# Reordering what stands ahead of the first attention scores in a transformer block with adaptive layer norm

## The chip, the cores and the metric

The kernel runs on one core of a Trainium2 chip. The metric is device time in microseconds (us) for one execution of the whole block, given as the median of several runs. A profiled execution has a span (first to last instruction) and a time of its own, which is a little longer than the span.

## The reference

Input x is 8 x 1024 x 256 in float32. The block computes, per batch:

```python
mod = (silu(c) @ wmod).reshape(8, 6, 1, 256)      # c: 8 x 256
sa, ca, ga, sb, cb, gb = ...                      # six rows; ga, gb kept at 0.25 or more in size
h = layernorm(x) * (1 + ca) + sa
x = x + ga * attention(h, w_qkv, w_o)             # 16 heads of 64, softmax over 1024 keys
h = layernorm(x) * (1 + cb) + sb
x = x + gb * ffn(h)                               # 8 experts, each takes its 512 best tokens
```

Only `h` of the first batch, its first projections (q, k, v) and the modulation rows stand ahead of the first attention scores, and the change is about these.

## The kernel before, in words

Attention is cut into units `u`: one batch, one pair of heads, one half of the queries (512). A unit has four groups `g`, and in each group two blocks of 128 keys are handled: TensorE makes the scores (`s`, L356), ScalarE copies them to SBUF (`p`, L365), VectorE keeps a running maximum (`top`, L370). At the end of the unit the maximum is turned (`tt`, L377), reduced and split in parts (L385 to L393), turned back (`pn`, L399) and spread (`less`, L412); in later groups VectorE subtracts it, ScalarE takes exp, TensorE multiplies with v (`av`, L427) and GpSimd adds up the denominators.

The order of every engine's instructions is written out by hand. `at(g, where, f, ...)` puts a small task into a group, and a loop over `g` (from -16 before) emits, for each group, loads, scores, the tasks of "m1", exp and values, and then the tasks of "m2". Small tasks are the projections `qk_task` (`pq`, L321, evicted by ScalarE to `qk`) and `v_task` (`pv`, L338), the turning of the normalised rows `ln_out` (`ptx`), `mod_rows` (`pr`, L229: four of the six rows of modulation, needed only much later), and the tasks of later stages. Groups below zero are the fill: no scores run there.

PSUM has four pools: `ps_s` with two tiles of two banks (tag "s", for scores and `tt`), `ps_b` (`less`), `ps_av` (`av`), and `ps_m` with one bank (tag "mm") which all small tasks share, one after the other. A tile is not written while another engine reads it, and the next task in a bank waits for the eviction of the one before.

Ahead of the loop stand the loads and the modulation. `c` (8 x 256), `wm0` (the third of wmod for sa and ca), and the rows of x of the first batch (two halves, `x_first`) are loaded on the SP queue; the weights of the first four heads (`wq0`, six loads of 128 KB) on ScalarE's queue; `late_loads` then puts the other heads' weights (`wq1`, six loads of 384 KB), the rest of wmod, w_o and small tensors on SP. A DMA takes one of eight semaphores in turn, and where one is used again the queue waits until the DMA that had it before has landed. `mod_silu` computes silu(c) from an exp on ScalarE and three operations on VectorE on 8 x 256, turns it in two blocks to `sT`, and `mod_columns` multiplies it with wm0 (`pm`, L215) into `modT`. `ln_first(t)` takes the statistics of 256 rows (VectorE, then a power on GpSimd) and normalises them on VectorE (L281). `ln_out` turns them with 16 passes of a matmul with the identity and evicts on VectorE, with modT as scale and shift (L300). `steps_of` is a small table used near the end of the kernel.

Of the kernel before, what the change touches and what calls it, by code (L numbers as in the profile page):

```python
# [32 lines left out]
ALU = mybir.AluOpType  # L33
# [9 lines left out]
def adaln_block(  # L43
# [51 lines left out]
    scores = const.tile([P, KT, E, NTT // KT], F32, name="scores")  # L95
    modT = const.tile([P, 2 * KC, B], F32, name="modT")


    steps_of = const.tile([P, 16, 4], I32, name="steps_of")
    nc.gpsimd.memset(steps_of, 0)  # L100
    nc.gpsimd.iota(steps_of[:, 14, :], pattern=[[1, 4]], base=0, channel_multiplier=0)
    for s in range(14):
        nc.vector.tensor_scalar(
            steps_of[:, s, :], steps_of[:, 14, :], 28 - 2 * s, None, op0=ALU.logical_shift_left
        )

    mod_d = dram.tile([B, 3 * D], F32, name="mod_d")
    gb_d = dram.tile([B, D], F32, name="gb_d")
# [45 lines left out]
    def wq_load(eng, i, a):  # L154
        heads = slice(0, H0) if i == 0 else slice(H0, H)
        for k in range(KC):
            eng.dma_start(
                wqs[i][:, k, a],
                w_qkv[heads, a, k * P : (k + 1) * P, :].rearrange("h p n -> p h n"),
            )  # L160
# [1 line left out]


    c_sb = small.tile([B, D], F32, tag="row", name="c_sb", bufs=6)
    nc.sync.dma_start(c_sb, c)
    wm = [work.tile([P, KC, 2 * D], F32, tag=t, name=f"wm{i}", bufs=n)
          for i, (t, n) in enumerate((("p", PB), ("ot", 2), ("ot", 2)))]

    def wm_load(i):
        nc.sync.dma_start(  # L170
            wm[i], wmod[:, 2 * i * D : 2 * (i + 1) * D].rearrange("(k p) m -> p k m", p=P)
        )

    wm_load(0)
    x_first = []
    for i in range(2):
        t = work.tile([P, NT // 2, D], F32, tag="p", name=f"x_first{i}", bufs=PB)
# [1 line left out]
            t, x[0, i * S // 2 : (i + 1) * S // 2, :].rearrange("(t p) d -> p t d", p=P)  # L179
        )  # L180
        x_first.append(t)
    for a in (2, 1, 0):
        wq_load(nc.scalar, 0, a)

    def late_loads():
        for a in (2, 1, 0):
            wq_load(nc.sync, 1, a)
        for i in (1, 2):
            wm_load(i)
        nc.sync.dma_start(wo, w_o.rearrange("(i p) d -> p i d", p=P))  # L190
        nc.sync.dma_start(rw, router_w.rearrange("(k p) e -> p k e", p=P))
        nc.sync.dma_start(rb, router_b.rearrange("(o e) -> o e", o=1).to_broadcast([P, E]))
        nc.sync.dma_start(b1_sb, b1.rearrange("e (f p) -> p e f", p=P))
# [3 lines left out]
    mod_row = []  # L197

    def mod_silu():
        sig = small.tile([B, D], F32, tag="row", name="sig", bufs=6)  # L200
        nc.scalar.activation(sig, c_sb, AF.Exp, scale=-1.0)
        nc.vector.tensor_scalar_add(sig, sig, 1.0)
        nc.vector.reciprocal(sig, sig)
        nc.vector.tensor_mul(sig, c_sb, sig)
        for k in range(KC):
            pt = ps_m.tile([P, B], F32, tag="mm", name=f"pt{k}")
            nc.tensor.transpose(pt, sig[:, k * P : (k + 1) * P], ident[:B, :B])
            nc.vector.tensor_copy(sT[:, k, :], pt)

    def mod_columns():  # L210

        pm = ps_m.tile([P, 2 * KC, B], F32, tag="mm", name="pm")
        for m in range(2 * KC):
            for k in range(KC):
                nc.tensor.matmul(  # L215
                    pm[:, m, :], wm[0][:, k, m * P : (m + 1) * P], sT[:, k, :],
                    start=(k == 0), stop=(k == KC - 1),
                )
        nc.vector.tensor_copy(modT[:, :KC, :], pm[:, :KC, :])
        nc.vector.tensor_scalar_add(modT[:, KC:, :], pm[:, KC:, :], 1.0)  # L220
# [31 lines left out]
    def at(g, where, f, *args):  # L252
        steps.setdefault((g, where), []).append((f, args))
# [5 lines left out]

    ln_x = {}  # L260

    def ln_load(b, t):
        ln_x[b, t] = small.tile([P, 2, D], F32, tag="lnx", name=f"lnx{b}_{t}", bufs=2)
        nc.sync.dma_start(
            ln_x[b, t], x[b, 2 * t * P : (2 * t + 2) * P, :].rearrange("(i p) d -> p i d", p=P)
        )
# [4 lines left out]
    def ln_first(t):  # L271
        ln_x[0, t] = x_first[t // 2][:, 2 * (t % 2) : 2 * (t % 2) + 2, :]
        ln_stats(0, t)
        ln_norm(0, t)

    def ln_norm(b, t):
        xt, mv = ln_x[b, t]
        rs = rstd_of(small, mv, 2, f"a{b}_{t}")
        for i in range(2):
            eng = nc.vector if b == 0 else nc.gpsimd  # L280
            eng.tensor_scalar(  # L281
                xt[:, i, :], xt[:, i, :], mv[:, i, 0:1], rs[:, i : i + 1],
                op0=ALU.subtract, op1=ALU.mult,
            )

    def ln_out(b, t):
        if t == 0:
            hTs[b] = work.tile([P, KC, S], F32, tag="hT", name=f"hT{b}")
        xt = ln_x.pop((b, t))[0]
        pt = ps_m.tile([P, KC, 2 * P], F32, tag="mm", name=f"ptx{b}_{t}")  # L290
        for k in range(KC):
            for i in range(2):
                for m in range(2):
                    c0 = k * P + m * N
                    nc.tensor.matmul(
                        pt[m * N : (m + 1) * N, k, i * P : (i + 1) * P],
                        xt[:, i, c0 : c0 + N], ident, start=True, stop=True,
                    )
        for k in range(KC):
            nc.vector.tensor_scalar(  # L300
                hTs[b][:, k, 2 * t * P : (2 * t + 2) * P], pt[:, k, :],
                modT[:, KC + k, b : b + 1], modT[:, k, b : b + 1],
                op0=ALU.mult, op1=ALU.add,
            )

    def ln_task(b, t, g):
        at(g - 4, "load", ln_load, b, t)
        at(g - 2, "post", ln_stats, b, t)
        at(g - 1, "pool", ln_norm, b, t)
        at(g, "m2", ln_out, b, t)  # L310


    def qk_task(b, p, i):
        a, half = (1, i) if i < 2 else (0, i - 2)
        if half == 0:
            qks[b, p, a] = work.tile([P, S], F32, tag="qk"[a], name=f"qk{a}_{b}_{p}")
        pq = ps_m.tile([P, 512], F32, tag="mm", name=f"pq{b}_{p}_{i}")
        sl = slice(half * 512, half * 512 + 512)
        for k in range(KC):
            for m in range(2):  # L320
                nc.tensor.matmul(  # L321
                    pq[m * N : (m + 1) * N, :], wq_of(k, a, 2 * p + m), hTs[b][:, k, sl],
                    start=(k == 0), stop=(k == KC - 1),
                )
        if a == 0:
            nc.scalar.mul(qks[b, p, a][:, sl], pq, scale)  # L326
        else:
            nc.scalar.copy(qks[b, p, a][:, sl], pq)  # L328
# [311 lines left out]
    def free_slot(g, behind=False):  # L640
# [2 lines left out]
        taken.add(g)  # L643
        return g

    for t in range(NT // 2):
        at(-15 + t, "m2", ln_out, 0, t)
        ln_task(1, t, free_slot(39 + 4 * t, True))
    for b in range(B):
        for p in range(NP):  # L650
            P0 = 8 * (b * NP + p)
            for i, g in enumerate((-7, -6, -5, -2)):
                at(P0 + g, "m1", qk_task, b, p, i)
            if p % 2 == 0:
                for t, g in enumerate((-9, -3, -1, 5)):
                    at(P0 + g, "m1", v_task, b, p // 2, t)
            if (b, p) == (B - 1, NP - 1):
                continue

            at(P0 + 17, "load", den_load, b, p)  # L660
            at(P0 + 18, "post", den_inv, b, p)
            at(P0 + 19, "load", den_spread, b, p)
            at(P0 + 20, "pool", den_mul, b, p)
        if b + 1 < B:
            if b + 2 < B:
                for t in range(NT // 2):
                    ln_task(b + 2, t, free_slot(64 * (b + 1) + 39 + 4 * t, True))
            for t in range(NT):
                g = free_slot(64 * (b + 1) + 19 + 4 * t, True)
                at(g - 2, "load", out_load, b, t)  # L670
                at(g, "m2", out_proj, ps_m, b, t)
                at(g + 1, "pool", out_norm, b, t)
                if t % 2:
                    g = free_slot(g + 2, True)
                    at(g, "m2", out_turn, ps_m, b, t - 1)
                    g = free_slot(g + 1)
                    at(g, "m2", out_route, ps_m, b, t - 1)
                    at(g + 1, "post", out_exp, b, t - 1)
                    at(g + 2, "post", out_score, b, t - 1)
                    at(g + 3, "pool", out_store, b, t - 1)  # L680
# [4 lines left out]
    for b in range(B):  # L685
        at(64 * b + 30, "load", gates, b)
    for i in range(2):
        at(-1, "m2", mod_rows, i)
    for t in range(NT):
        at(4 * NSU + (3 if t < NT // 2 else 4), "load", last_load, t)  # L690

    with tc.manual_schedule():
        late_loads()
        mod_silu()
        ln_first(0)
        mod_columns()
        for t in range(1, NT // 2):
            ln_first(t)
        for t in parts_of:
            nc.vector.memset(t, 0.0)  # L700
        g = -16
        while g < 4 * NSU + LAG or steps:
            u, gm = divmod(g, 4)
            run(g, "load")
# [88 lines left out]
                out_store(b, s - 4)  # L793
    assert not steps, sorted(steps)
    attn.close()


    wts = ctx.enter_context(tc.tile_pool(name="ewts", bufs=4))
    ex_w = {}
# [281 lines left out]
```

## Time and profile before

| | |
|---|---|
| median of 3 runs | 3637.75 us (3636.31 to 3641.64) |
| profiled execution, its time | 3636.69 us |
| its span | 3635.0 us |
| mean granted TensorE clock | 0.983 |
| TensorE busy | 3462.8 us (95%) |
| VectorE busy | 2904.0 us (80%) |
| GpSimd busy | 2657.6 us (73%) |
| ScalarE busy | 2432.8 us (67%) |
| first scores on TensorE start | 59.89 us |

Busy time is the time in which an engine has an instruction in work; matmuls overlap, so a busy TensorE is not one at its peak. PE is TensorE, PEld its weight loads, ACT ScalarE, DVE VectorE, POOL GpSimd, SP SyncE (which only issues DMAs). A line of the timeline gives start, length, engine, source line, operation, tiles and number of records; the bracket tells how long the engine was idle before and what ended it. The row of 40 digits gives busy tenths of equal slices of 91 us.

### The profile page before, as it was taken

How to read it: one execution, taken by the hardware profiler on the slowest of the kernel's cores; microseconds unless marked ns; L12 is line 12 of the kernel's file. 1: busy time of each engine (PE TensorE's matmuls, PEld its weight loads, DVE VectorE, ACT ScalarE, POOL GpSimd, SP SyncE). 2: the span in 40 equal slices, each digit the busy share in tenths (PEclk: the TensorE clock that was granted, in tenths of full speed). 3: DMA queues.
4: the chain of work that ended last, by engine and by line, in shares of the span. 5: the costliest groups of instructions: out<-in, count | busy, mean ns of one | idle time of the engine just before them, and what ended most of it. 6: DMA issues, size and time to landing. Idle time of an engine off the chain costs nothing. (4 is left out here: it accounts for less than half of the span.)

```text
span 3635.0 us, 54304 instructions
## 1 busy us (share of the span) xinstructions
PE 3462.8 (95%) x20670; PEld 1460.7 (40%) x20670; DVE 2904.0 (80%) x3651; ACT 2432.8 (67%) x2980; POOL 2657.6 (73%) x1537
## 2 busy tenths in 40 slices
PE   6999999999999999999999999999999999982898
PEld 2333334334433434334433344344334344342565
DVE  4888888888888888888888888888888888857442
ACT  2777777777777777777777777777777777740111
POOL 0778778887788777977788888877888887851232
PEclk9999999999999999999999999999999999995999
DMA  3010011111121122111211112011311112133332
GB/s 76 13 38 29 24 31 57 45 43 41 49 56 38 45 61 55 33 39 45 65 52 30 52 45 62 30 52 43 62 38 43 46 51 56 51 85 122 94 99 41
DMA packets 189653, 185.40 MB, mean 51 GB/s; under 512 B 48952, under 2 KB 167240, under 8 KB 189264
## 3 DMA queue, kind: packets, MB, share of 16 engines
q1 hardware_dynamic: 170736, 160.04, 15.6%
q0 software_dynamic: 7168, 12.72, 1.8%
q10 hardware_dynamic: 11488, 9.18, 0.9%
q8 instruction: 163, 2.67, 0.3%
q14 instruction: 98, 0.80, 0.1%
HBM read 127.06 MB, written 63.21 MB: 52 GB/s over the span
## 5 line engine op out<-in xcount | busy, mean ns | idle before, releaser
L446 POOL TENSOR_TENSOR acc<-acc,p 128x1024 f32<-128x1024 f32 x762 | 1805.2, 2369 | 361.8 <-ACT p L418 328.5
L365 ACT COPY p<-s 128x1024 f32<-128x1024 f32 x1024 | 996.2, 1018 | 421.1 <-PE s L356 414.5
L415 DVE TENSOR_TENSOR p<-p,less 128x1024 f32<-128x1024 f32 x1024 | 1206.7, 1210 | 32.8 <-PE less L412 30.0
L370 DVE TENSOR_TENSOR top<-top,s 128x1024 f32<-128x1024 f32 x768 | 936.9, 1220 | 259.9 <-ACT p L365 218.2
L418 ACT ACTIVATE p<-p 128x1024 f32<-128x1024 f32 x1024 | 1041.7, 1057 | 75.0 <-DVE p L415 74.7
L356 PE MATMUL s<-qk,qk 64*128 64x512 f32 x4096 | 1024.9, 612 | 36.1 <-DVE parts L393 32.3
L427 PE MATMUL av<-p,v 128*64 128x512 f32 x4096 | 968.1, 593 | 1.8 <-ACT oT L436 1.8
L356 PEld LDWEIGHTS s<-qk,qk 64*128 64x128 f32 x4096 | 358.3, 186 | 528.7 <-issue 240.1
L321 PE MATMUL pq<-hT,wq 128*64 128x512 f32 x2048 | 495.9, 605 | 2.7 <-ACT qk L328 1.4
L427 PEld LDWEIGHTS av<-p,v 128*64 128x64 f32 x4096 | 280.6, 137 | 461.9 <-issue 367.3
L443 POOL TENSOR_TENSOR acc<-p,p 128x1024 f32<-128x1024 f32 x127 | 301.6, 2375 | 190.4 <-ACT p L418 190.4
L321 PEld LDWEIGHTS pq<-hT,wq 128*64 128x64 f32 x2048 | 124.1, 136 | 343.0 <-issue 211.4
L338 PE MATMUL pv<-wq,hT 128*64 128x256 f32 x2048 | 251.0, 387 | 2.6 <-ACT qk L326 1.4
L1006 ACT ACTIVATE h<-ph,b_sb 128x512 f32<-128x512 f32 x64 | 44.0, 687 | 274.6 <-PE ph L1002 274.6
L385 DVE TENSOR_REDUCE tt<-tt 128x8 f32<-128x1024 f32 x128 | 157.4, 1230 | 67.7 <-PE tt L377 67.6
L537 PE MATMUL po<-wo,ot 128*64 128x256 f32 x1792 | 205.7, 382 | 0.0
L338 PEld LDWEIGHTS pv<-wq,hT 128*64 128x64 f32 x2048 | 136.4, 137 | 155.5 <-issue 66.2
L370 DVE TENSOR_TENSOR top<-p,s 128x1024 f32<-128x1024 f32 x128 | 155.9, 1218 | 9.8 <-ACT p L365 9.8
L343 ACT COPY v<-pv 128x512 f32<-128x512 f32 x128 | 74.9, 585 | 129.7 <-PE pv L338 129.7
L377 PEld LDWEIGHTS tt<-ident,top 128*128 128x128 f32 x1024 | 109.6, 140 | 107.2 <-DVE top L370 107.2
L508 POOL TENSOR_TENSOR oT<-oT,rb 128x1024 f32<-128x1024 f32 x63 | 149.9, 2380 | 3.3 <-DMA rb<-rden_d 3.3
L537 PEld LDWEIGHTS po<-wo,ot 128*64 128x64 f32 x1792 | 123.5, 137 | 66.2 <-issue 9.4
(166 smaller groups left out, 2429.7 us busy)
## 6 DMA issues: line engine op xcount, KB each, us to landing
rb<-rden_d SPq DMA_DIRECT2D x128, 256.0 KB
oT_d<-oT SPq DMA_DIRECT2D x62, 512.0 KB
ot<-oT_d SPq DMA_DIRECT2D x56, 512.0 KB
rows_d<-row SPq DMA_DIRECT2D x64, 132.0 KB
rows_d<-gb_d SPq DMA_DIRECT2D x8, 1024.0 KB
w<-in_L_ffn_w_dram ACTq DMA_DIRECT2D x8, 1024.0 KB
w<-in_L_ffn_w_dram SPq DMA_DIRECT2D x8, 1024.0 KB
lnx<-in_L_attn_inputs_dram SPq DMA_DIRECT2D x28, 256.0 KB
```

The source lines that it names most:

```text
L321: nc.tensor.matmul(pq[m * N : (m + 1) * N, :], wq_of(k, a, 2 * p + m), hTs[b][:, k, sl], start=(k == 0), stop=(k == KC - 1),)
L338: nc.tensor.matmul(pv[m * N : (m + 1) * N, i, :], hTs[b][:, k, t0 : t0 + N], wq_of(k, 2, 4 * g, 4), start=(k == 0), stop=(k == KC - 1),)
L356: nc.tensor.matmul(ps[:, j, :], kt[r, c * P : (c + 1) * P], qt[r, h * QB : (h + 1) * QB], start=True, stop=True,)
L365: nc.scalar.copy(probs[u, c], ps)
L370: nc.vector.tensor_tensor(tops[u], probs[u, 0] if c == 1 else tops[u], ps, ALU.max)
L385: nc.vector.tensor_reduce(nm[:, 0, :], tt, AX.X, ALU.max, negate=True)
L415: nc.vector.tensor_tensor(probs[u, c], probs[u, c], less[u], ALU.add)
L418: nc.scalar.activation(probs[u, c], probs[u, c], AF.Exp)
L427: nc.tensor.matmul(avs[u][j * N : (j + 1) * N, :], v[:, c, hh * N : (hh + 1) * N], pT[:, j, :], start=(c == 0), stop=(c == NT - 1),)
L443: nc.gpsimd.tensor_tensor(sums[u], pts[0], pts[1], ALU.add)
L446: nc.gpsimd.tensor_tensor(sums[u], sums[u], pt, ALU.add)
L537: nc.tensor.matmul(po[m * N : (m + 1) * N, :], ot[:, p, m * N : (m + 1) * N], wo[:, p, :], start=(p == 0), stop=(p == NP - 1),)
```

## The change

- Loads: `c` and `wm0` go on ScalarE's queue, so that SP's own list has the rows of x at its head; the six `wq0` loads stand behind the exp on ScalarE's queue, in the order k, q, v; `late_loads` is called behind them.
- silu: `c` itself is turned (two blocks into one tile), and exp, add, reciprocal and multiply run on the turned 128 x 16.
- `pm` has the bank of `av`.
- `ln_out` of the first batch turns with four transposes of 128 x 128 and evicts on ScalarE, with modT as scale and bias.
- `bank(...)`: the first two turns and the projections `pq` 0 and 2 of the first pair of heads use the scores' two-bank tiles.
- Tasks: the loop starts at g = -2. In front of the first scores stand turns 0 and 1, `pq` 0 and 2, turns 2 and 3, `pq` 1 and `pv` 0; `pq` 3, `pv` 1 and 2 and the two `mod_rows` go into groups 0 to 3.
- Norms and statistics are interleaved by one tile; `steps_of` is made behind them.

```diff
     c_sb = small.tile([B, D], F32, tag="row", name="c_sb", bufs=6)
-    nc.sync.dma_start(c_sb, c)
+    nc.scalar.dma_start(c_sb, c)
...
-    wm_load(0)
+    wm_load(nc.scalar, 0)
...
-    for a in (2, 1, 0):
-        wq_load(nc.scalar, 0, a)
...
     def mod_silu():
-        sig = small.tile([B, D], F32, tag="row", name="sig", bufs=6)
-        nc.scalar.activation(sig, c_sb, AF.Exp, scale=-1.0)
-        nc.vector.tensor_scalar_add(sig, sig, 1.0)
-        nc.vector.reciprocal(sig, sig)
-        nc.vector.tensor_mul(sig, c_sb, sig)
+        pt = ps_m.tile([P, KC, B], F32, tag="mm", name="pt")
         for k in range(KC):
-            pt = ps_m.tile([P, B], F32, tag="mm", name=f"pt{k}")
-            nc.tensor.transpose(pt, sig[:, k * P : (k + 1) * P], ident[:B, :B])
-            nc.vector.tensor_copy(sT[:, k, :], pt)
+            nc.tensor.transpose(pt[:, k, :], c_sb[:, k * P : (k + 1) * P], ident[:B, :B])
+        nc.scalar.activation(sT, pt, AF.Exp, scale=-1.0)
+        nc.vector.tensor_scalar_add(sT, sT, 1.0)
+        nc.vector.reciprocal(sT, sT)
+        nc.vector.tensor_mul(sT, sT, pt)
...
-        pm = ps_m.tile([P, 2 * KC, B], F32, tag="mm", name="pm")
+        pm = ps_av.tile([P, 2 * KC, B], F32, tag="av", name="pm")
...
+    def bank(shape, name, start=False):
+
+        if start:
+            return ps_s.tile(shape, F32, tag="s", name=name)
+        return ps_m.tile(shape, F32, tag="mm", name=name)
...
-        pt = ps_m.tile([P, KC, 2 * P], F32, tag="mm", name=f"ptx{b}_{t}")
+        pt = bank([P, KC, 2 * P], f"ptx{b}_{t}", (b, t) in ((0, 0), (0, 1)))
+        if b == 0:
+            for k in range(KC):
+                for i in range(2):
+                    nc.tensor.transpose(
+                        pt[:, k, i * P : (i + 1) * P], xt[:, i, k * P : (k + 1) * P], ident
+                    )
+                nc.scalar.activation(
+                    hTs[b][:, k, 2 * t * P : (2 * t + 2) * P], pt[:, k, :], AF.Identity,
+                    bias=modT[:, k, b : b + 1], scale=modT[:, KC + k, b : b + 1],
+                )
+            return
...
-        pq = ps_m.tile([P, 512], F32, tag="mm", name=f"pq{b}_{p}_{i}")
+        pq = bank([P, 512], f"pq{b}_{p}_{i}", (b, p) == (0, 0) and i % 2 == 0)
...
     for t in range(NT // 2):
-        at(-15 + t, "m2", ln_out, 0, t)
+        at(-2 if t < 2 else -1, "m1", ln_out, 0, t)
...
+    for i, g in ((0, -2), (2, -2), (1, -1), (3, 0)):
+        at(g, "m1", qk_task, 0, 0, i)
+    for t, g in enumerate((-1, 0, 1)):
+        at(g, "m1", v_task, 0, 0, t)
...
     for i in range(2):
-        at(-1, "m2", mod_rows, i)
+        at(2 + i, "m2", mod_rows, i)
...
     with tc.manual_schedule():
+        mod_silu()
+        for a in (1, 0, 2):
+            wq_load(nc.scalar, 0, a)
         late_loads()
-        mod_silu()
         ln_first(0)
+        ln_first(1)
+        ln_norm(0, 0)
         mod_columns()
-        for t in range(1, NT // 2):
+        for t in range(2, NT // 2):
             ln_first(t)
+            ln_norm(0, t - 1)
+        ln_norm(0, NT // 2 - 1)
         for t in parts_of:
             nc.vector.memset(t, 0.0)
-        g = -16
+
+        nc.gpsimd.memset(steps_of, 0)
...
+        g = -2
```

In the built program SP's first DMA is one load of `wq1`; the two halves of x follow it, then the other `wq1` loads.

More of the change, by code (lines that the diff above doesn't have):

```diff
@@ L99, in adaln_block @@
     steps_of = const.tile([P, 16, 4], I32, name="steps_of")
[L100 to L105, printed above, removed]
     mod_d = dram.tile([B, 3 * D], F32, name="mod_d")
@@ L164, in adaln_block, with wm_load @@
     c_sb = small.tile([B, D], F32, tag="row", name="c_sb", bufs=6)
-    nc.sync.dma_start(c_sb, c)
+    nc.scalar.dma_start(c_sb, c)
     wm = [work.tile([P, KC, 2 * D], F32, tag=t, name=f"wm{i}", bufs=n)
           for i, (t, n) in enumerate((("p", PB), ("ot", 2), ("ot", 2)))]
-    def wm_load(i):
-        nc.sync.dma_start(
+    def wm_load(eng, i):
+        eng.dma_start(
             wm[i], wmod[:, 2 * i * D : 2 * (i + 1) * D].rearrange("(k p) m -> p k m", p=P)
         )
-    wm_load(0)
+    wm_load(nc.scalar, 0)
     x_first = []
@@ L188, in late_loads @@
         for i in (1, 2):
-            wm_load(i)
+            wm_load(nc.sync, i)
         nc.sync.dma_start(wo, w_o.rearrange("(i p) d -> p i d", p=P))
@@ L273, in ln_first @@
         ln_stats(0, t)
-        ln_norm(0, t)
     def ln_norm(b, t):
@@ L652, in adaln_block @@
             for i, g in enumerate((-7, -6, -5, -2)):
-                at(P0 + g, "m1", qk_task, b, p, i)
+                if P0:
+                    at(P0 + g, "m1", qk_task, b, p, i)
             if p % 2 == 0:
                 for t, g in enumerate((-9, -3, -1, 5)):
-                    at(P0 + g, "m1", v_task, b, p // 2, t)
+                    if P0 or g > 0:
+                        at(P0 + g, "m1", v_task, b, p // 2, t)
             if (b, p) == (B - 1, NP - 1):
@@ L692, in adaln_block @@
     with tc.manual_schedule():
+        mod_silu()
+        for a in (1, 0, 2):
+            wq_load(nc.scalar, 0, a)
         late_loads()
-        mod_silu()
         ln_first(0)
+        ln_first(1)
+        ln_norm(0, 0)
         mod_columns()
-        for t in range(1, NT // 2):
+        for t in range(2, NT // 2):
             ln_first(t)
+            ln_norm(0, t - 1)
+        ln_norm(0, NT // 2 - 1)
         for t in parts_of:
             nc.vector.memset(t, 0.0)
-        g = -16
+        nc.gpsimd.memset(steps_of, 0)
+        nc.gpsimd.iota(steps_of[:, 14, :], pattern=[[1, 4]], base=0, channel_multiplier=0)
+        for s in range(14):
+            nc.vector.tensor_scalar(
+                steps_of[:, s, :], steps_of[:, 14, :], 28 - 2 * s, None, op0=ALU.logical_shift_left
+            )
+        g = -2
         while g < 4 * NSU + LAG or steps:
```

## The prediction

> **What bounds the kernel now.** I read the page's busy shares first, then TensorE's timeline of the first 75 us, then ScalarE's and the SP queue's, because the change touches only what stands ahead of the first scores.
>
> ```profile
> PE 3462.8 (95%) x20670; PEld 1460.7 (40%) x20670; DVE 2904.0 (80%) x3651; ACT 2432.8 (67%) x2980; POOL 2657.6 (73%) x1537
> PE   6999999999999999999999999999999999982898
> ```
>
> TensorE is busy in 95% of the span, and its first slice (91 us) is the one low slice before the end. So time is bought in the fill, and a shift there should reach the end undiminished: behind it every engine runs the same instructions in the same order in both kernels. The last common point that I use is the start of the first max_rows (`pn`, L399), at 80.66 us before: everything that TensorE does up to there is done in both kernels up to there.
>
> ```profile
> 11.98 3.58 PE L215 MATMUL pm<-sT,wm 128*128 128x8 f32 x16 [0.26 <-DVE sT L208]
> 26.00 1.98 PE L295 MATMUL ptx<-ident,x_first 128*64 128x128 f32 x16 [8.06 <-DVE hT L300]
> 35.42 3.66 PE L338 MATMUL pv<-wq,hT 128*64 128x256 f32 x16 [1.18 <-DVE hT L300]
> 39.76 1.94 PE L321 MATMUL pq<-hT,wq 128*64 128x512 f32 x8 [0.67 <-ACT v L343]
> 47.63 1.95 PE L338 MATMUL pv<-wq,hT 128*64 128x256 f32 x16 [0.70 <-ACT qk L326]
> 58.08 1.88 PE L229 MATMUL pr<-wm,sT 128*8 128x512 f32 x4 [0.66 <-ACT mrow L232]
> 59.89 1.99 PE L356 MATMUL s<-qk,qk 64*128 64x512 f32 x8
> ```
>
> The reader sees three stages: the modulation (to 15.9 us), four turns of h (to 35.3; the second waits 8 us for VectorE, which does all four norms before the first eviction), and nine tasks in one PSUM bank, each of 1.9 us of matmul and 0.7 us of eviction (to 59.9). The first `pv` takes 3.66 us and a later one 1.95: TensorE is at half clock until 38.93 us, where the clock records begin with full speed.
>
> ```profile
> 0.80 4.78 ACTq L157 DMA_DIRECT2D wq<-in_L_attn_w_qkv_dram  x6
> 6.91 0.41 ACT L201 ACTIVATE sig<-c_sb 8x256 f32<-8x256 f32 x1
> 7.67 1.74 DVE L203 RECIPROCAL sig<-sig 8x256 f32<-8x256 f32 x1
> 25.05 0.81 DVE L300 TENSOR_SCALAR hT<-ptx,modT 128x256 f32<-128x256 f32 x2
> 1.72 1.84 SPq L178 DMA_DIRECT2D x_first<-in_L_attn_inputs_dram  x2
> ```
>
> By the DMA semaphores c landed at 2.50, wm0 at 5.84, the halves of x at 8.45 and 11.16, and the six wq1 loads from 13.57 to 22.26: only the norms ever waited for data.
>
> **The change part by part.**
>
> *silu.* c is turned first (landed 2.5, two turns 0.5 us), and ACT issues only two DMAs (0.4 each) and the table load (1.28) ahead of exp. Exp, add and multiply on 128x16 cost about 0.2 each, the reciprocal 0.25 (the 128x16 row of L488) for 1.74. sT stands at about 4.3 instead of 11.9. What is late next is wm0: it shares the DMA engines with the first wq1 load, I put it at 6.0. `pm` then takes its 3.6 cold, modT stands near 9.9 for 15.9.
>
> *Loads.* In the built order SP does not begin with x: one wq1 load (384 KB of 256-byte packets) stands ahead of both halves. Those packets moved 218 GB/s and 1 KB packets about 370, so it costs 1.8 us of the DMA engines, about what the earlier wq0 loads took from x before. I put x at 8.4 and 10.4: no gain there. First stats and norm (two stats each 0.4 and 0.18; POOL 1.0; two norms 0.73), with the second tile's stats between them, end at 11.7.
>
> *The wait that is new.* The six wq0 loads now stand on ACT behind exp, and each reuses a DMA semaphore: the third waits for wm0, the fourth and fifth for the halves of x, the sixth for the third wq1 load. ACT's next work is the eviction of the turns, which moved there from DVE, so it stands behind that sixth issue. Up to the third wq1 load go 1.84 MB in 256-byte packets (8.4 us at 218), x (1.05 MB, 2.8 us) and wm0 (2.3 us, as slow as it was): with 2 us ahead and the landing, 15.3, and 0.5 for the issue. ACT is free at 15.8. Bounds: 11.8 if the semaphores come early (norm and modT then decide), 17.5 if an issue takes the 1.7 us that the sixth took before.
>
> *Two turns.* Per 128-row half, two transposes (cold about 0.6; the eight of L377 take 1.09 warm) and an ACT eviction of 128x256. That with scale and bias is not in the trace; the nearest is the 128x256 copy of L470, 0.37; I take 0.4, at most the 0.52 of DVE's L300. One PSUM tile is not written while it is read, so the steps are serial: about 2.4 us from 15.8 until the first projection starts at 18.2 with its first half of k.
>
> *Two projections, in two of the scores' banks.* 3.9 us of warm work without an eviction between them. Half clock lasted 3.5 us from the start of the first dense stretch before; as the clock moves in steps of 3.41 us I allow 3.4 to 6.8, take 5.1, and get 3.9 + 2.5 = 6.4: to 24.6.
>
> *The other two turns* share one bank: four times (0.45 + 0.4 + two handovers) plus the q eviction in front, 4.1 us: to 28.7. Then `pq` and `pv` with an eviction between, 1.94 + 0.7 + 1.95: the first scores start at 33.3 for 59.89.
>
> *What comes back in the scores.* `pq` 1.94, two `pv` 3.90, two `pr` 3.76 now lie between the first scores and `pn`: 9.6 us. They fill 1.8 us of the waits that stood there (1.41 on DVE's top, 1.25 on parts), so this stretch takes 20.8 + 9.6 - 1.8 = 28.6, and `pn` starts at 61.9 for 80.66. POOL has no sums to add up yet. The nine small DVE operations on mrow (2.8 us) now delay the next top by 0.2. steps_of's memset, iota and 14 operations of 0.15 go behind the norms where DVE has nothing until the first top (at 36); if that cover failed they would cost 1.1.
>
> Sum: 80.66 - 61.9 - 0.2 = 18.6 us.
>
> **A rule against it.** The Trainium skill ("TensorE: Matmul & The Clock Gate", Part 1) says that the clock falls to half after at least one idle window of about 3.4 us. Here a window need not be idle:
>
> ```profile
> 3216.74:3220.15 3.41, 1.61 (x22) 0.69 (x18) 3.38 (x6) 3.34 (x6) 3.33 (x2) 1.00 0.03 4
> 3220.15:3223.57 3.42, 3.42 (x18) 0.70 (x20) 3.35 (x9) 3.35 (x4) 0.53 (x3) 0.50 0.06 14
> ```
>
> After 1.61 us of TensorE work in 3.41 (47%) the next window ran at half, while windows with 59% kept full speed. The stretch with the two later turns has 42% in 4.1 us. By the rule nothing is lost (18.6); by the trace a window falls under the limit about every second time, and one or two windows at half cost 1.7 to 3.4. I take half of 2.5: 17.4 us.
>
> The profiled execution took 3636.69 (span 3635.0 and 1.7 around it), 1.06 below the median 3637.75. 3636.69 - 17.4 = 3619.3, and with the 1.06 the forecast is 3620.3.
>
> **The rivals.** *ACT is not held.* Third wq1 load and issue early, ACT free at 11.8: 4 us more, about 3616. For it: ACT's own ring is nearly empty. Against: SP's issues took 1.7 to 3.4 us each from 6.3 on, with its queue full. Chance 0.10.
>
> *The gain is eaten by banks.* Up to g = 3 a v or q task waits for ACT behind two 1.0-us copies. I counted 0.6 for two of them; if all seven moved or remaining tasks wait 1.6, 7 us go, and with re-throttling nearly 10: about 3629. Chance 0.07; a total near no change needs 18 and has 0.03.
>
> *Slower: the clock does not come up.* If the short stretches, each ended by an eviction, never fill a 3.41-us window, TensorE stays at half through the first unit. The 34 us of warm work between the turns and `pn` would then take up to 30 us more: 3620.3 + 28 = about 3648. It decides from about 60 us on: half clock until there uses up the whole gain. For it: windows with 58 to 61% (25 to 35 us) did not raise the clock. Against: at half clock the work doubles and the waits do not, so a full window comes soon, as with the first `pv`. Chance 0.03.
>
> **How the numbers follow.** My forecast, with or without the re-throttled window, has 0.77. Range 3614 to 3629: below it the ACT rival at full size, above it the bank rival's tail and the slow clock. A measurement of this kernel tells 0.2% (7.3 us) from no change. Faster by more needs under 3630.5: 0.94; same 0.03; slower 0.03.
>
> **What would show it.** The first hT eviction on ACT at about 15.8, right behind the sixth wq0 issue; the first `s` at 33 and `pn` at 62; full clock from 21.6 to 25; perhaps one window at half near 28. An eviction at 12 is the first rival; `pn` over 70 says that a step here is mis-sized; a shift at `pn` that is not found again at the end says that the fill is not what carries.

## The result, and the profile after

The changed kernel took 3620.67 us in the median of five runs (3620.46 to 3623.01), the kernel before 3637.75 in the median of five (3636.31 to 3642.11): a ratio of 0.9952, 95% interval 0.9938 to 0.9967. The forecast was 3620.3 with a range from 3614 to 3629.

The profiled execution after took 3623.01 us for a span of 3621.3, at a mean clock of 0.982. It is the slowest of its five runs, 2.34 us above their median, so the gain read from the two traces (13.7 us of span) is smaller than that of the medians (17.1). Busy shares and the 40 slices of TensorE:

```profile
PE 3462.3 (96%) x20622; PEld 1457.6 (40%) x20622; DVE 2898.7 (80%) x3641; ACT 2436.6 (67%) x2988; POOL 2658.8 (73%) x1537
PE   7999999999999999999999999999999999982898
```

TensorE's busy time is within 0.5 us of what it was (3462.8). What became less is idle time in the first slice, whose busy share rose from 6 to 7 tenths. ScalarE's queue comes next, because the forecast hung on it (start, length, engine, line; ACTq is the queue's own issue of DMAs):

```profile
3.18 0.18 ACT L194 ACTIVATE sT<-pt 128x16 f32<-128x16 f32 x1
3.39 12.43 ACTq L150 DMA_DIRECT2D wq<-in_L_attn_w_qkv_dram  x5
15.44 0.37 ACTq L150 DMA_DIRECT2D wq<-in_L_attn_w_qkv_dram  x1
15.92 0.56 ACT L291 ACTIVATE hT<-ptx,modT 128x256 f32<-128x256 f32 x1 [12.56 <-DVE x_first L275]
```

The 12.43 us of the second line are the last five wq0 loads. They are mostly waits between issues: the fifth was issued at 9.78, the sixth (the third line, from a narrower window) at 15.44. The eviction behind it began 0.11 us after the end of that issue. The bracket names DVE's x_first, but what the eviction needs of DVE (the norm of the first tile, and modT behind it) stood at 11.07, and the turn had ended at 11.44; the name in the bracket is not what held it. In the built order the sixth issue has the semaphore of the third wq1 load, and that load landed at 15.42 by its semaphore events.

On VectorE's and SP's timelines, the reciprocal and the issue of x stand at

```profile
3.61 0.25 DVE L196 RECIPROCAL sT<-sT 128x16 f32<-128x16 f32 x1
1.30 1.49 SPq L171 DMA_DIRECT2D x_first<-in_L_attn_inputs_dram  x2
```

where before they took 1.74 and 1.84 us. TensorE's timeline up to the first scores, and then the first `pn`:

```profile
6.44 3.55 PE L204 MATMUL pm<-sT,wm 128*128 128x8 f32 x16 [3.52 <-DMA wm<-in_L_wmod_dram]
16.54 1.11 PE L288 MATMUL ptx<-ident,x_first 128*128 128x128 f32 x4 [5.10 <-ACT hT L291]
18.96 5.76 PE L326 MATMUL pq<-hT,wq 128*64 128x512 f32 x16
25.88 0.44 PE L288 MATMUL ptx<-ident,x_first 128*128 128x128 f32 x2 [0.79 <-ACT hT L291]
28.06 0.44 PE L288 MATMUL ptx<-ident,x_first 128*128 128x128 f32 x2 [0.66 <-ACT hT L291]
29.16 2.83 PE L326 MATMUL pq<-hT,wq 128*64 128x512 f32 x8 [0.65 <-ACT hT L291]
32.66 3.68 PE L343 MATMUL pv<-wq,hT 128*64 128x256 f32 x16 [0.68 <-ACT qk L333]
36.27 2.27 PE L361 MATMUL s<-qk,qk 64*128 64x512 f32 x8
65.34 0.41 PE L404 MATMUL pn<-ident_b,parts 128*64 128x128 bf16 x8
```

The first scores start 23.6 us earlier (36.27 for 59.89). Between there and `pn` lie 29.07 us instead of 20.77, because the tasks that were taken out of the fill now stand there. So `pn` is 15.3 us earlier (65.34 for 80.66), and the last `pn` of the kernel, at 3197.42 for 3212.17, still 14.75: a shift in the fill does reach the end.

A `pq` of 2.83 us and a `pv` of 3.68 stand where warm ones take 1.94 and 1.95. The clock says why. The table by stretches (from:to, length, then busy us and count for PE, PEld, DVE, ACT, POOL, then the granted clock, the DMA share and GB/s), cut along the edges of its own windows of 3.41 us:

```profile
23.23:26.65 3.42, 2.30 (x12) 0.68 (x8) 0.00 (x0) 1.39 (x4) 0.00 (x0) 1.00 1.11 339
26.65:30.06 3.41, 1.78 (x8) 0.74 (x10) 0.00 (x0) 1.39 (x3) 0.00 (x0) 1.00 1.62 17
30.06:33.48 3.42, 2.74 (x10) 0.77 (x8) 0.00 (x0) 0.58 (x1) 0.00 (x0) 0.50 0.26 1
33.48:36.89 3.41, 3.41 (x16) 1.70 (x14) 0.00 (x0) 0.50 (x1) 0.00 (x0) 0.50 0.00 0
```

The window with 1.78 us of TensorE work in 3.41 (52%) holds the second of the two later turns and the start of a `pq`, and it is followed by two windows at half clock.

### The profile page after: what moved, and what is told of

Read it like the earlier page. It is cut to its first block, busy times and chain, and to the rows that moved or that the text cites. A ratio compares the mean times of both kernels' runs of the same rounds, so it can differ in the third digit from the quotient of the medians.

```text
span 3621.3 us, 54202 instructions
## 1 busy us (share of the span) xinstructions
PE 3462.3 (96%) x20622; PEld 1457.6 (40%) x20622; DVE 2898.7 (80%) x3641; ACT 2436.6 (67%) x2988; POOL 2658.8 (73%) x1537
## 5 line engine op out<-in xcount | busy, mean ns | idle before, releaser
L382 PE MATMUL tt<-ident,top 128*128 128x128 f32 x1024 | 139.9, 280 | 3.3 <-DVE top L375 3.3
```

What stands on the lines that cost most here:

```text
L382: nc.tensor.transpose(turned[u][:, 4 * j + t, :], top[:, j, t * P : (t + 1) * P], ident)
```

## The experiments

Times are medians, with the ratio to the kernel before in runs on the same chip. That kernel took 3638.19 us beside e1 to e4, 3636.9 beside e5 to e8 and 3637.36 beside e9 and e10.

**e1: the v weights go through SP.** ScalarE keeps four wq0 loads; the two that waited longest are issued on SP. In the built order one of them heads SP's list, where the change has a wq1 load of three times its size, and the other follows x.

```diff
-        for a in (1, 0, 2):
+        for a in (1, 0):
             wq_load(nc.scalar, 0, a)
+        wq_load(nc.sync, 0, 2)
```

> The changed kernel with the two v loads of wq0 moved from ScalarE's queue to SP's. Theory (ScalarE is held by the sixth wq0 issue until 15.8 us): ScalarE is left with four issues, the last behind a half of x, and is free at about 10; the first eviction of a turn starts at about 11.2 instead of 15.9, the first projection at about 14.5 instead of 19.0, and the time falls by about 4 us to some 3616.5. Rival (the hold covers another wait that ends as late, in the norms or in the data): the first eviction stays within 1 us of 15.9 and the time at 3620 to 3623.

Measured: 3616.0 us, ratio 0.9937 (0.992 to 0.9953). ScalarE's timeline:

```profile
3.25 6.00 ACTq L150 DMA_DIRECT2D wq<-in_L_attn_w_qkv_dram  x4
11.35 0.57 ACT L291 ACTIVATE hT<-ptx,modT 128x256 f32<-128x256 f32 x1 [7.92 <-PE ptx L288]
```

The queue is free at 9.25, and the eviction follows the turn, at 11.35 for 15.92. The turn itself ends when it did with the change (11.31 for 11.44), so the other order on SP did not bring this. `pn` stands at 58.97, 6.37 us earlier than with the change: 4.57 of them at this eviction, the other 1.8 at the clock, which stays at half for one window instead of two:

```profile
21.43:24.85 3.42, 1.45 (x7) 0.60 (x8) 0.00 (x0) 1.70 (x3) 0.00 (x0) 1.00 1.02 372
24.85:28.26 3.41, 2.78 (x8) 0.48 (x4) 0.00 (x0) 0.59 (x1) 0.00 (x0) 0.50 1.13 241
```

The medians differ by 4.7. So the hold on ScalarE was real, and it cost about as much as the rival "ACT is not held" had put on it (4 us).

**e2: the change with silu as before.**

```diff
-        pt = ps_m.tile([P, KC, B], F32, tag="mm", name="pt")
+        sig = small.tile([B, D], F32, tag="row", name="sig", bufs=6)
+        nc.scalar.activation(sig, c_sb, AF.Exp, scale=-1.0)
...
+            nc.tensor.transpose(pt, sig[:, k * P : (k + 1) * P], ident[:B, :B])
+            nc.vector.tensor_copy(sT[:, k, :], pt)
```

> The changed kernel with silu as it was (on 8 x 256, then turned). The silu chain is about 3 us longer, sT at 7.4 instead of 4.2, and modT at about 11.3. But with one wait less the semaphores of the DMAs fall differently: the sixth wq0 load reuses that of the first half of x (7.8 us) and not that of the third wq1 load. Theory (the hold on ScalarE decides): free at about 8.5, first eviction at 11.5, and the kernel with the slower silu is 4 us faster than the changed one, about 3616.5. Rival (silu's chain decides): first eviction 3 us later than 15.9, time up by 3 us; if silu is merely hidden, 15.9 and no change.

Measured: 3616.79 us, ratio 0.994 (0.9924 to 0.9957): 3.9 us less than the change's median although silu is slower. sT is copied from 6.56 on (the change has it at 4.14), but the change's product waited for wm0 until 6.44, so little is lost there: the product starts at 6.98. What is gained lies in the queue:

```profile
2.33 0.93 ACTq L150 DMA_DIRECT2D wq<-in_L_attn_w_qkv_dram  x2
3.29 6.24 ACTq L150 DMA_DIRECT2D wq<-in_L_attn_w_qkv_dram  x4
11.38 0.57 ACT L293 ACTIVATE hT<-ptx,modT 128x256 f32<-128x256 f32 x1 [7.78 <-PE ptx L290]
```

With another order of issues the eight semaphores fall differently: in the built order the sixth wq0 load now has that of the first half of x instead of the third wq1 load's, and the queue is free at 9.53. With all six loads on it, ScalarE was free 6.3 us earlier than with the change. It is the wait for a reused semaphore that held ScalarE, not the number of issues.

**e3: the turns and tasks of the change, with loads and silu as before.**

```diff
-    nc.scalar.dma_start(c_sb, c)
+    nc.sync.dma_start(c_sb, c)
...
-        mod_silu()
-        for a in (1, 0, 2):
-            wq_load(nc.scalar, 0, a)
         late_loads()
+        mod_silu()
```

> The kernel before with the new order of tasks, the banks, transposes and ScalarE's evictions, but its own loads, silu and place of them. Theory (in the changed kernel the hold gives back what the loads and silu saved): modT stands at 15.9 as before, ScalarE is free at 7.3, the first eviction starts at about 16.1, so the whole gain is there without the loads and silu: 3620.5, within 2 us of the changed kernel. Rival (the parts add up): loads and silu brought some 5 of the 17 us, and this is at 3625 to 3626.

Measured: 3620.54 us, ratio 0.9946 (0.9929 to 0.9962), the time of the whole change (3620.67). sT is complete at 10.65 (4.14 with the change), but the first eviction is 1.4 us *earlier* than with the change, right behind its turn:

```profile
14.52 0.57 ACT L295 ACTIVATE hT<-ptx,modT 128x256 f32<-128x256 f32 x1 [7.53 <-PE ptx L292]
```

Put on top of the new turns, the new loads and silu bring nothing: the hold at the sixth issue gives all of it back.

**e4: the loads and silu of the change in the kernel before.**

```diff
-    nc.sync.dma_start(c_sb, c)
+    nc.scalar.dma_start(c_sb, c)
...
-        late_loads()
         mod_silu()
+        for a in (1, 0, 2):
+            wq_load(nc.scalar, 0, a)
+        late_loads()
```

> The kernel before with the new loads and silu only, its order of tasks and VectorE's evictions kept. The statistics of x start at 7.9 instead of 11.85, the norms end at about 19.7 instead of 24.6, and everything behind them comes 4 to 5 us earlier: first scores at 55, time 3633. Rival (loads and silu carry most of the gain): modT is 5 us earlier and x comes first, first scores at 45 to 50, time about 3625. Rival (nothing): the four norms and turns hide it, 3637.

Measured: 3633.2 us, ratio 0.9987 (0.9979 to 0.9994): about 5 us less than the kernel before. Here DVE evicts, so nothing on the path stands behind ScalarE's queue. The first eviction of h comes 3.6 us earlier (21.41 for 25.05), the first `pv` 3.7 earlier. At `pn` 1.9 are left in the profiled executions, because the clock came up later (40.17 for 38.93) and a cold `pq` stands behind the cold `pv`. The time was as expected, but not by the way that was expected: the first scores are at 57.99, not at 55, and of the 5 us between the medians only 2.1 stand in the two profiled spans.

**e5: TensorE is kept busy between the later turns**, by four transposes of the identity into a bank that nobody reads, behind each half of the turns of tiles 2 and 3. This is work added that the kernel doesn't need.

```diff
+                if t >= 2:
+                    idle = ps_b.tile([P, 2, QB], F32, tag="less", name=f"idle{t}_{k}")
+                    for i in range(4):
+                        nc.tensor.transpose(idle[:, 0, i * P : (i + 1) * P], ident, ident)
```

> The changed kernel with four dummy transposes of the identity (0.55 us) after each pair of transposes of turns 2 and 3, into a bank that is free, so that TensorE works through the evictions. Theory (the two windows at half clock, 30.06 to 36.89 in the changed kernel's profile, come from the 50% window of these turns and cost 3.4 us): the clock stays at full speed once it is up, the first scores start at about 33.3 instead of 36.3, pn at 62 instead of 65.3, and the profiled execution falls by some 3 us to 3620. Rival (the drop has another cause, or the dummies cost what they save): a half-speed window stands in the clock records again, pn stays at 65 or later.

Measured: 3617.22 us, ratio 0.9945 (0.993 to 0.9961), with an outlier of 3620.76 in four runs. The timeline of the same stretch, and the two windows of the later turns:

```profile
24.21 0.60 PE L298 MATMUL idle<-ident 128*128 128x128 f32 x4
28.44 1.94 PE L330 MATMUL pq<-hT,wq 128*64 128x512 f32 x8 [0.22 <-ACT hT L291]
31.06 1.95 PE L347 MATMUL pv<-wq,hT 128*64 128x256 f32 x16 [0.69 <-ACT qk L337]
```

```profile
22.02:25.43 3.41, 3.06 (x18) 1.33 (x15) 0.00 (x0) 1.64 (x3) 0.00 (x0) 1.00 1.07 368
25.43:28.84 3.41, 2.75 (x20) 1.84 (x20) 0.00 (x0) 1.69 (x3) 0.00 (x0) 1.00 1.46 129
28.84:32.26 3.42, 2.73 (x20) 1.12 (x18) 0.00 (x0) 0.58 (x1) 0.00 (x0) 1.00 0.88 10
```

With 90% and 81% in the windows the clock stays, `pq` and `pv` take 1.94 and 1.95, and `pn` comes at 61.72 instead of 65.34. The clock also came up earlier than with the change (22.02 for 23.24), and the later turns start 0.7 us earlier (23.93 for 24.65). The other 2.9 of the 3.6 us at `pn` lie behind that start: this is what the re-throttling was worth. Idle TensorE time in short gaps has a price here, and useless work removes it.

**e6: x stands at the very head of SP's queue**, ahead of the first wq1 load.

```diff
     with tc.manual_schedule():
+        x_load()
         mod_silu()
```

> The changed kernel with both halves of x really at the head of SP's list, ahead of all wq1 loads. Theory (the hold on ScalarE hides the data): x lands at 6.3 instead of 7.8, but the sixth wq0 issue now waits for the second wq1 load, at about 13.5, so the first eviction starts at about 14 and the gain is these 2 us, about 3618.5, not the norms' 1.5. Rival (x decides): norms and everything behind them come 1.5 us earlier and no more. Rival: no change at all, 3620.7.

Measured: 3617.23 us, ratio 0.9941 (0.9926 to 0.9957). The first half of x lands at 4.91 instead of 7.84 and the statistics start at 4.94, yet the first eviction is at 13.54:

```profile
13.54 0.56 ACT L295 ACTIVATE hT<-ptx,modT 128x256 f32<-128x256 f32 x1 [9.37 <-DMA wq<-in_L_attn_w_qkv_dram]
```

The landing of wm0 is pushed back from 6.31 to 8.04, and the sixth wq0 issue now waits for the second wq1 load, which landed at 13.04. The early x itself isn't used. What came was that hold, 2.4 us shorter than with the change, and one window at half clock (26.96 to 30.37) instead of two.

**e7: e1, with the small tasks spread over more PSUM banks.** Every half of a turn has its own tile, and turns, `pq`, `pv` and `pr` of the first groups alternate between the banks of `s`, `less`, `av` and `mm`, so that none waits for the eviction of the one before.

```diff
+    first = {
+        "ptx0_0_0": "s", "ptx0_0_1": "s", "ptx0_1_0": "less", "ptx0_1_1": "mm",
+        "pq0_0_0": "s", "pq0_0_2": "av",
...
-        pt = bank([P, KC, 2 * P], f"ptx{b}_{t}", (b, t) in ((0, 0), (0, 1)))
...
+                pt = bank([P, 2 * P], f"ptx{b}_{t}_{k}")
```

> The kernel with the v loads on SP, and in addition: each half of a turn has a bank of its own, and the small tasks up to the first values alternate between two banks. Theory (with the hold gone, the fill is bound by evictions between tasks of one bank, and by the half clock that these gaps bring): turns 2 and 3 take 2.5 us instead of 4.5, no task waits 0.7 us for its bank, no window at half clock; first scores at about 26.3 instead of 30.2, pn at 53 instead of 59, time 3610. Rival (ScalarE, which makes all evictions, is then the bound): pn at 57 or later, 3614 to 3616.

Measured: 3608.3 us, ratio 0.9917 (0.9902 to 0.9932), 7.7 us less than e1.

```profile
8.05 3.55 PE L204 MATMUL pm<-sT,wm 128*128 128x8 f32 x16 [5.03 <-DMA wm<-in_L_wmod_dram]
20.32 1.09 PE L296 MATMUL ptx<-ident,x_first 128*128 128x128 f32 x8
22.91 1.94 PE L335 MATMUL pq<-hT,wq 128*64 128x512 f32 x8 [1.50 <-ACT hT L299]
24.68 1.90 PE L352 MATMUL pv<-wq,hT 128*64 128x256 f32 x16
26.50 1.99 PE L370 MATMUL s<-qk,qk 64*128 64x512 f32 x8
```

The later turns run as one piece of 1.09 us, and behind them only the third `pq` waits in front of the scores, 1.50 us for the last eviction. No window of this stretch is under 71%, and the clock never falls. From the first `pq` to `s` it takes 11.7 us (15.6 in e1), from `s` to `pn` 26.2 (28.8). The start is not better: the first eviction is at 12.16 (11.35 in e1), because wm0 landed at 7.92 for 7.10. The loads are those of e1, so the banks did not bring this.

**e8: e7, with x at the head of SP as in e6, half of the later evictions on VectorE, and `steps_of` made in group 3.**

```diff
+                if t >= 2 and k == 1:
+                    nc.vector.tensor_scalar(
+                        hTs[b][:, k, 2 * t * P : (2 * t + 2) * P], pt,
+                        modT[:, KC + k, b : b + 1], modT[:, k, b : b + 1],
...
+    at(3, "post", steps_table)
...
+        x_load()
```

> All together: v loads on SP behind x, x at the head, banks as in the last kernel, and half of the later turns' evictions on VectorE, the small table made later. First eviction at about 10 instead of 11.3, first scores at 24, pn at 50.5, time about 3608. Rival (wm0 and pm, which is 3.6 us at half clock, decide the start): first eviction stays at 11.3 and the time at 3610.

Measured: 3607.25 us, ratio 0.9915 (0.9902 to 0.9929). The first eviction stayed at 12.0, as the rival had it. x was there early and the first tile was normalised at 7.99, but

```profile
7.89 3.56 PE L208 MATMUL pm<-sT,wm 128*128 128x8 f32 x16 [3.93 <-DMA wm<-in_L_wmod_dram]
22.20 1.94 PE L346 MATMUL pq<-hT,wq 128*64 128x512 f32 x8 [0.75 <-DVE hT L304]
```

wm0, behind x on the DMA engines, landed at 7.75. Only the split eviction showed: the third `pq` waits 0.75 us instead of 1.50.

**e9: e8, with wm0 at the head of SP's queue, ahead of x.**

```diff
-    wm_load(nc.scalar, 0)
...
+        wm_load(nc.sync, 0)
         x_load()
         mod_silu()
```

> The kernel of e8 with the load of the modulation's weight (wm0) moved from ScalarE's queue to the head of SP's queue, ahead of x; ScalarE issues c alone. Theory (wm0's landing and the modulation's product behind it decide the start): wm0 lands near 5 us instead of 7.75, the product ends near 8.7, the first eviction into hT is near 10 instead of 12.0, the first scores near 24 instead of 25.8, the first deferred normalisation near 50, the time near 3605.5. Rival (x, which now starts behind wm0 and lands near 6.4 or later, and the norms decide): first eviction at 11.5 or later, time 3607 or more.

Measured: 3604.91 us (3604.52 to 3605.49), ratio 0.9911 (0.9894 to 0.9927).

```profile
4.88 3.56 PE L207 MATMUL pm<-sT,wm 128*128 128x8 f32 x16 [1.20 <-DMA wm<-in_L_wmod_dram]
8.96 1.23 PE L299 MATMUL ptx<-ident,x_first 128*128 128x128 f32 x4 [0.53 <-DVE x_first L286]
23.68 1.99 PE L380 MATMUL s<-qk,qk 64*128 64x512 f32 x8
49.88 0.41 PE L423 MATMUL pn<-ident_b,parts 128*64 128x128 bf16 x8
```

The first eviction is at 9.80, `pn` 2.1 us earlier than in e8 (51.99), the profiled time 2.1 us lower (3604.52 for 3606.65). The theory's numbers held (10, 24, 50 and 3605.5). Now the turn waits 0.53 us for the norm once the product has ended, so the two loads are nearly balanced. It is the fastest of the kernels here, about 16 us under the changed one.

**e10: the kernel before with the new turns alone.**

```diff
-        ln_norm(0, t)
...
+        if b == 0:
+            for k in range(KC):
+                for i in range(2):
+                    nc.tensor.transpose(
+                        pt[:, k, i * P : (i + 1) * P], xt[:, i, k * P : (k + 1) * P], ident
+                    )
...
+        ln_first(1)
+        ln_norm(0, 0)
         mod_columns()
```

> The kernel before with one part of the change alone: the turns ahead of the projections (half the transposes at a time, ScalarE's eviction with the modulation in it, norms in between), all in one bank; tasks, loads and silu as before. Theory (turns and deferral of tasks share the gain): first eviction near 15.6, eight half-steps of about 1.35 us at the low clock, so turned x is ready near 26.4 instead of 35.3, first scores near 51 instead of 59.9, time near 3629. Rival (the deferral of tasks carries nearly all): 3634 or more. Rival (the turns carry nearly all): 3624 or less.

Measured: 3629.17 us, ratio 0.9977 (0.9967 to 0.9986).

```profile
19.82 0.69 PE L293 MATMUL ptx<-ident,x_first 128*128 128x128 f32 x2 [0.66 <-ACT hT L296]
26.54 3.42 PE L348 MATMUL pv<-wq,hT 128*64 128x256 f32 x16 [0.66 <-ACT hT L296]
50.78 1.99 PE L366 MATMUL s<-qk,qk 64*128 64x512 f32 x8
```

Each half-turn takes 0.69 and waits 0.66, and the first `pv` starts at 26.54 for 35.42. `pn` is at 71.56, 9.1 us earlier than before. e3, which has the tasks moved and spread over banks as well, is another 7.5 us earlier (64.08). By the medians it is 8.2 us for e10 and 17.7 for e3. So the turns carry about half of the gain, the tasks and their banks the rest, and neither rival holds.

## Why the prediction was right, step by step

| step | forecast | measured in the change |
|---|---|---|
| third wq1 load lands | 15.3 | 15.42 |
| first eviction of h | 15.8 | 15.92 |
| first `pq` starts | 18.2 | 18.96 |
| first two `pq` end | 24.6 | 24.7 |
| turns 2 and 3 end | 28.7 | 29.1 |
| first `s` | 33.3 | 36.27 |
| from `s` to `pn` | 28.6 | 29.07 |
| `pn` | 61.9 | 65.34 |

The forecasts of the last rows are those before the allowance for re-throttling (1.25 us), which the prediction took off at the end.

**The wait that is new** was the main term, and it held: the sixth wq0 issue behind the third wq1 load, to 0.1 us (the terms that it prints, 8.4, 2.8, 2.3 and 2, make 15.5 and not 15.3; the load landed between). e1 and e2 take it away in two ways, and each gains. That silu and the loads bring nothing beside it is what e3 adds; the prediction had not said it.

**The eviction** was undersized. It was taken at 0.4, from a 128x256 copy of 0.37; with scale and bias it took 0.56, a little over the upper bound of 0.52. Three of them stand ahead of the first `pq`, and they explain about half of the 0.8 us by which it was late. The two `pq` made it up: they took 5.76 instead of 6.4, because the clock came up at 23.24, within the forecast's 21.6 to 25.

**The re-throttling** was the step that failed in size. The prediction weighed the Trainium skill's rule ("TensorE: Matmul & The Clock Gate", Part 1: half clock after an idle window) against the trace and took half of 2.5 us. The clock fell to half in all five profiles that have the later turns with these gaps: in the change and e3, two windows; in e1, e2 and e6, one. The windows in front of it had 42 to 52% of TensorE work, not none. In the change it cost 2.9 us, by e5; without it, the forecast for `pn` (61.9, and 0.2) stands against 61.72 in e5. That rule speaks of idle windows only, and here the measurement decides.

**The sum.** The forecast was a gain of 17.4 us. The profiled executions show 15.3 at `pn`, 14.75 at the last `pn` and 13.7 in span. The medians show 17.1. Of the 3.7 us between 17.4 and 13.7, 2.1 stand at `pn`, and 1.65 of these are the rest of the re-throttling (2.9 for 1.25). Another 0.6 is lost between the first and the last `pn`, for a cause that stays open. The last 1.0 lies behind the last `pn`, where the change took 423.8 us for 422.8, and it is the clock again. The first product of the experts starts 162.8 us behind the last `pn` in both kernels, but the clock comes back to full speed 2.2 us after its start in the kernel before (first line) and 4.6 with the change (second line):

```profile
3374.93 4.79 PE L1002 MATMUL ph<-xT,w 128*128 128x512 f32 x8
3360.26 5.98 PE L1026 MATMUL ph<-xT,w 128*128 128x512 f32 x8
```

So a gain in the fill arrives at the end with a part added or taken away that has nothing to do with the fill: in the twelve profiles this product takes 4.6 to 6.2 us, the longer the later the clock rises (1.8 to 5.1 us after its start), and the eight that have a window at half clock near 3200 us come to this product 1.3 to 1.9 us later behind the last `pn` than e5, e7, e8 and e9, which have none. That is why e5's span is 6.8 us below that of the change, with only 3.6 of it at `pn`.

The medians came out nearer because the profiled run of the change lies 2.34 us above its own median, and that of the kernel before 1.06 below. The runs of the change lie at 3620.5 to 3620.7 (three) and 3622.7 to 3623.0 (two). Such steps of the clock would be of this size, but only the profiled run has a clock record here, so that stays open. The forecast time is closer than its terms were: that it lies within 0.4 us of the median is in part luck.

**The rivals.** "ACT is not held" would have given 3616; e1, which makes it true, gave 3616.0. "The gain is eaten by banks" was wrong in size for the change: three tasks between `s` and `pn` wait 0.7 us each (e7, without these waits, is 2.9 us shorter there), and the stretch was forecast to within 0.5. "The clock does not come up" did not happen: it came up at 23.24 in the change and by 24 in all kernels with the new order of tasks.

**A reading that was off.** The prediction has the first half of x landing at 8.45 before. By its semaphore that is a wq0 load, and the half of x landed at 8.11. With the change it landed at 7.84, not at 8.4; behind the hold on ScalarE this made no difference.

## What to carry to other kernels

A DMA issue on a compute engine's queue may wait for the semaphore of a quite unrelated load, and all that the engine computes next waits with it. So look in the built order at what each issue waits for, keep such issues off an engine that is soon needed, and recheck it after any edit of the order of loads (e2 was faster with a slower silu).

Where a short stage runs on TensorE at full clock, count its work by windows of 3.41 us: here windows with 42 to 52% of work were followed by one or two at half clock, and giving each small task its own PSUM bank saved both the gaps and the clock.

When several loads must all be there before the first product, order them by the length of what follows each of them: moving only x to the front (e6, e8) pushed wm0 back, and the start moved only when wm0 went first (e9).

## What the runs showed of the hardware that was not expected

- Windows with 42 to 52% of TensorE work were followed by half clock in each of the five profiles that have them between the later turns, and windows of 47 to 50% near 3200 us in eight of the twelve; in e5 and e7 none of the fill's windows behind the rise, up to `pn`, was under 71%, and the clock stayed. The share alone doesn't decide: windows of 45% (the change, from 3245.42) and 48% (e7, from 3189.75) kept the full clock. It decides the rise still less. After a window of 80 or 81% the clock came back in e1, e2 and e6, and it did not in the change (from 30.06) and e3; and a window that the modulation's products, of 8 columns each, filled to 100% did not raise it in e1, e2, e7 and e8.
- The landing of wm0 is the last of 16 events on its semaphore, and that one can be late. e4 has the loads of the change, and wm0 landed at 8.14 for 6.31, with fifteen events by 6.65; in e7 it was 7.92, with fifteen by 7.01. What is loaded ahead shifts all of them: the eighth of them came at 5.87 with the change, at 7.31 with x at the head of SP (e6), and at 4.53 with wm0 itself there (e9, landed at 4.74).
- ScalarE's eviction of 128x256 with scale and bias took 0.56 us, a plain copy of the same shape 0.37.
